# Expert tiles of a mixture-of-experts stage: one of each expert, then pairs on one load of weights, then singles, with the sums in two tables

## The chip, the cores and the metric

The kernel runs on one core of one Trainium2 chip. The metric is the time of one execution on the device, in microseconds (us). Three runs of the kernel before took 2542.0, 2550.27 and 2550.65 us; their median is 2550.27 us.

## What is computed

Two graph-attention stages and two feed-forward stages are run in turn on 3125 rows of 256 numbers, each with a layer norm in front and a residual behind it. The change lies in the second one, a mixture of 16 experts of which every row uses two, and at the border to the third, three graph-attention layers:

```python
def _L0_ffn_ref(x, gate_w, gate_b, w1, w2, w3):
    logits = jnp.einsum('bsd,de->bse', x, gate_w) + gate_b
    probs = jax.nn.softmax(logits, axis=-1)
    top_probs, top_idx = jax.lax.top_k(probs, 2)
    top_probs = top_probs / jnp.sum(top_probs, axis=-1, keepdims=True)
    dispatch = jnp.sum(jax.nn.one_hot(top_idx, n_experts, dtype=x.dtype) * top_probs[..., None], axis=-2)
    h1 = jnp.einsum('bsd,edh->bseh', x, w1)
    h2 = jnp.einsum('bsd,edh->bseh', x, w2)
    hidden = jax.nn.silu(h1) * h2
    expert_out = jnp.einsum('bseh,eho->bseo', hidden, w3)
    return jnp.einsum('bseo,bse->bso', expert_out, dispatch)
...
x = x + _L0_gnn_ref(_layernorm(x, axis=-1), ...)
x = x + _L0_ffn_ref(_layernorm(x, axis=-1)[None], ...)[0]
x = x + _L1_gnn_ref(_layernorm(x, axis=-1), ...)
x = x + _L1_ffn_ref(_layernorm(x, axis=-1)[None], ...)[0]
```

Here the model width is 256, an expert's hidden width is 512, and all of it is float32.

## The kernel before

Rows are held in 25 blocks of 128 (`NB`), and five blocks make a chunk (`NCH` is 5). The program is written with a framework that places instructions on each engine's queue by a model of its own, takes care of all waits, and hands out buffers from pools; where the source opens a `manual_schedule`, an engine keeps the written order. Each engine works through its own queue in order. DMAs are issued from the queues of SP, ACT and POOL.

**First graph layer (L550 to L719).** For each chunk and head, ACT and DVE make the choice matrices `t`, `m` and `m2` (L577 to L589) and PE multiplies them with the features (L593). They lie in the pool `m0` together with smaller tiles such as `red`, `total` and `gate_w`. At its end the residual rows are written to a table `x_d` in HBM and the normalised rows to `xn_d`.

**Routing (L736 to L958).** The gate's logits are made by PE, and DVE finds each row's two experts. From L858 on, DVE works in written order: `running` (L870) forms running sums by doubling steps, `pre` the rows of each expert before each block. From these come the number of 128-row tiles per expert, the expert of each tile (`owner`, L898), and every row's `place`. The two gate weights of each row are written as 8-byte pieces into `xn_d` by ACT (L924). One-hot matrices `slot`, `give` (L934, L939) and 2 x 25 matmuls into `pslot` (L942) turn places into lists: `token` (L955), the row number of each slot, and `target` (L958), where its result goes.

**Experts (L960 to L1019).** The 56 tiles (`MU`) of up to 128 rows are run one after the other, in the order of the experts. For each tile SP reads the tile's expert into a register (L967) and loads that expert's `w1`, `w2` and `w3` of 512 KB each (L976, L978, L980; six buffers each). POOL gathers the rows `xg` from `xn_d` (L982); PE transposes them (`pt`, L136) and ACT copies them (`xT`, L138); PE makes `h1` and `h2` (L991), ACT the silu (L995), DVE the product `hid` (L996), PE the output `po` (L999), DVE the weighted `yo` (L1005, three buffers). POOL then adds `yo` into the rows `target` of `x_d` with an indirect DMA (L1006). Ahead of the fifth tile `later_weights` (L830) loads the next layers' attention vectors on ACT's queue (L839) and DVE multiplies them in (L844). If the routing needs more than 56 tiles, branches behind the loop (L1014, L1017) run the rest. Then ACT loads the five chunks of `x` back from `x_d` (L1021).

**Start of the next graph layer (L1025 to L1139), called the feed below.** POOL loads `wr`, `br`, `fw1`, `fw2`, `fb2` and `b1r`, the bias of the last stage (L1102), which PE transposes (L1104) and DVE copies (L1105). `lengths` (L1112) makes the statistics of a chunk on DVE and ACT (L1117 to L1126); then each block is normalised (`rows`, L1134), transposed and multiplied by the layer's weights (`ph`, L1089, copied by ACT, L1090). Three layers follow that stream all pairs of nodes through ACT, DVE and PE (L1325, L1327, L1336).

Of the kernel before, what the change touches and what calls it, by code (L numbers as in the profile page):

```python
# [9 lines left out]
F32 = mybir.dt.float32  # L10
I32 = mybir.dt.int32
BF16 = mybir.dt.bfloat16
AF = mybir.ActivationFunctionType
OP = mybir.AluOpType
AX = mybir.AxisListType
PSUM = bass.MemoryType.PSUM

P = 128
N = 3125
NB = 25  # L20
NP = NB * P
# [16 lines left out]
MT = 64  # L38
MU = 2 * N // P + NE // 2
# [45 lines left out]
def network(ctx: ExitStack, tc: tile.TileContext, ins, out, flag):  # L85
# [10 lines left out]
    x_d = nc.dram_tensor("x_d", (NP + P, D), F32, kind="Internal").ap()  # L96

# [452 lines left out]
    with tc.tile_pool(name="m0a", bufs=1) as ap, tc.tile_pool(name="m0", bufs=2) as mp, tc.tile_pool(  # L550
# [21 lines left out]
        def produce(dc, h, s, state):  # L572
            if s == 0:
                state["row"] = heads.pop(0) if heads else head_row(dc, h)
            row, k = state["row"], s % CH
            at = tiles[dc, s // CH]
            if k == 2:  # L577
                m = mp.tile([P, CW], BF16, name="m", bufs=2)
                nc.vector.scalar_tensor_tensor(m, row, nleft[:, s, h : h + 1], at[:, k, :], op0=OP.is_ge, op1=OP.mult)  # L579
                return m  # L580

            if k in (0, 3):
                state["t"] = mp.tile([P, 2, CW], BF16, name="t")
                state["m"] = mp.tile([P, 2, CW], BF16, name="m2", bufs=3)
            t, m, i = state["t"], state["m"], k in (1, 4)
            nc.scalar.activation(t[:, int(i), :], row, AF.Relu, bias=steep[:, s, h : h + 1], scale=STEEP)  # L586
            if i:
                nc.vector.tensor_tensor(m, t, at[:, k - 1 : k + 1, :], OP.min)  # L588
            return m[:, int(i), :]  # L589
# [200 lines left out]
        with tc.manual_schedule(engines={mybir.EngineType.DVE, mybir.EngineType.Activation}):  # L790
# [7 lines left out]
            for b in range(NB):  # L798
# [4 lines left out]
                xt = mp.tile([P, 2, CW], BF16, name="t").rearrange("p k t -> p (k t)").bitcast(F32)  # L803
# [46 lines left out]
    with tc.tile_pool(name="mo", bufs=1) as mo:  # L850
        owner = mo.tile([P, MT], I32, name="owner")
        used = mo.tile([P, 1], I32, name="used")
# [5 lines left out]
        with tc.tile_pool(name="mg", bufs=1) as mg, tc.tile_pool(name="mg1", bufs=1, space=PSUM) as ps1, tc.manual_schedule(  # L858
# [3 lines left out]
            nc.sync.dma_start(x_d[NP:, :], clear)  # L862

# [6 lines left out]
            def running(tot, a, bb, n):  # L870
# [3 lines left out]
                while step < n:  # L874
# [7 lines left out]
            fullt = mg.tile([P, NE], F32, name="fullt")  # L882
            nc.vector.tensor_scalar(fullt, pre[:, NB - 1, :], float(P - 1), None, op0=OP.add)
            tiles_i = mg.tile([P, NE], I32, name="tiles_i")
            nc.vector.tensor_copy(tiles_i, fullt)
            nc.vector.tensor_scalar(tiles_i, tiles_i, 7, None, op0=OP.arith_shift_right)
            tiles = mg.tile([P, NE], F32, name="tiles")
            nc.vector.tensor_copy(tiles, tiles_i)
            end = running(tiles, mg.tile([P, NE], F32, name="end0"), mg.tile([P, NE], F32, name="end1"), NE)

            nc.vector.tensor_copy(used, end[:, NE - 1 :])
            which = mg.tile([P, MT, NE], F32, name="which")
            nc.gpsimd.iota(which, pattern=[[1, MT], [0, NE]], base=0, channel_multiplier=0,
                           allow_small_or_imprecise_dtypes=True)
            nc.vector.tensor_tensor(which, which, end[:, None, :].to_broadcast([P, MT, NE]), OP.is_ge)
            own = mg.tile([P, MT], F32, name="own")
            nc.vector.tensor_reduce(own, which, AX.X, OP.add)
            nc.vector.tensor_scalar(owner, own, float(NE - 1), None, op0=OP.min)  # L898

            base = mg.tile([P, NE], F32, name="base")  # L900
            nc.vector.tensor_sub(base, end, tiles)
            nc.vector.tensor_scalar(base, base, float(P), None, op0=OP.mult)
# [3 lines left out]
            nc.vector.tensor_add(where, where, base[:, None, :].to_broadcast(ex3))  # L906
# [22 lines left out]
            for i in range(2):  # L929
# [11 lines left out]
                for b in range(NB):  # L941
                    nc.tensor.matmul(pslot, hot[0][:, b // 2, :, b % 2], give[:, b // 2, :, :, b % 2],  # L942
                                     start=(i == 0 and b == 0), stop=(i == 1 and b == NB - 1))
            second = mg.tile([P, MT], F32, name="second")
# [15 lines left out]
        def experts(first, last, ew, deep):  # L960

            with tc.tile_pool(name="ep", bufs=2, space=PSUM) as ps:
                w3_loads = []
                for i in range(first, last):
                    if first == 0 and i == 4:
                        later_weights(ew, busy)
                    loads, (e,) = nc.values_load_multi_w_load_instructions(  # L967
                        owner[0:1, i : i + 1], engines=[mybir.EngineType.SP], min_val=0, max_val=NE - 1)
                    if i >= first + 2:

                        tc.add_manual_dep(
                            loads[0].ins, w3_loads[i - first - 2].ins.name,
                            mybir.DependencyInfo(mybir.DependencyClass.NoSync, mybir.DependencyReason.SCHED_ONLY),
                            reason="registers")
# [5 lines left out]
                    w3_loads.append(nc.sync.dma_start(w3, ins["L0_ffn_w3"][ds(e, 1)].rearrange("o (k p) h -> p (o k) h", p=P)))  # L980
                    xg = ew.tile([P, D + 2], F32, name="xg", bufs=6)
                    nc.gpsimd.indirect_dma_start(  # L982
                        out=xg, out_offset=None, in_=xn_d,
                        in_offset=bass.IndirectOffsetOnAxis(ap=token[:, i : i + 1], axis=0))
                    xt = transposed(ps, ew, xg)
                    hs = []
                    for w, name in ((w1, "h1"), (w2, "h2")):
                        ph = ps.tile([P, HID // P, P], F32, name=name)
                        for f in range(HID // P):
                            for k in range(2):  # L990
                                nc.tensor.matmul(ph[:, f, :], w[:, k, f * P : (f + 1) * P], xt[:, k, :],  # L991
                                                 start=(k == 0), stop=(k == 1))
                        hs.append(ph)
                    hid = ew.tile([P, HID // P, P], F32, name="hid")
                    busy = nc.scalar.activation(hid, hs[0], AF.Silu)  # L995
                    nc.vector.tensor_mul(hid, hid, hs[1])  # L996
                    po = ps.tile([P, D], F32, name="po")
                    for f in range(HID // P):
                        nc.tensor.matmul(po, hid[:, f, :], w3[:, f, :], start=(f == 0), stop=(f == HID // P - 1))  # L999
                    share = ew.tile([P, 1], F32, name="share")  # L1000
                    nc.vector.tensor_mul(share, xg[:, D + 1 :], turn[1][:, i : i + 1])  # L1001
                    nc.vector.scalar_tensor_tensor(share, xg[:, D : D + 1], turn[0][:, i : i + 1], share,
                                                   op0=OP.mult, op1=OP.add)
                    yo = ew.tile([P, D], F32, name="yo")
                    nc.vector.tensor_scalar(yo, po, share, None, op0=OP.mult)  # L1005
                    nc.gpsimd.indirect_dma_start(  # L1006
                        out=x_d, out_offset=bass.IndirectOffsetOnAxis(ap=target[:, i : i + 1], axis=0),
                        in_=yo, in_offset=None, compute_op=OP.add)


        experts(0, MU, ew0, 6)
        early.close()
        count = nc.values_load(used[0:1, 0:1], min_val=0, max_val=MT)
        with tc.If(count > MU):  # L1014
            with tc.tile_pool(name="ew2", bufs=2) as ew:
                experts(MU, MU + 2, ew, 2)
            with tc.If(count > MU + 2):  # L1017
                with tc.tile_pool(name="ew3", bufs=3) as ew:
                    experts(MU + 2, MT, ew, 3)  # L1019
        for g in range(NCH):  # L1020
            nc.scalar.dma_start(x[:, g * CH : (g + 1) * CH, :],  # L1021
                                x_d[g * CW : (g + 1) * CW, :].rearrange("(b p) c -> p b c", p=P))
# [52 lines left out]
    with tc.tile_pool(name="g1", bufs=1) as g1, tc.tile_pool(name="g1w", bufs=2) as gw, tc.tile_pool(  # L1075
# [24 lines left out]

        b1r = gw.tile([P, NP - CW], BF16, name="rjunk").bitcast(F32)[:NF, :P]
        nc.gpsimd.dma_start(b1r, ins["L1_ffn_b1"].rearrange("(f p) -> f p", p=P))  # L1102
        pr = ps.tile([P, 512], F32, name="ph")
        nc.tensor.transpose(pr[:, :NF], b1r, ident[:NF, :NF])  # L1104
        nc.vector.tensor_copy(fb1, pr[:, :NF])  # L1105
# [177 lines left out]
        with tc.tile_pool(name="g1l", bufs=3) as gm:  # L1283
            for layer in range(3):
# [17 lines left out]
                nc.vector.tensor_scalar(bp, q, SLOPE - 1.0, -HALF, op0=OP.mult, op1=OP.add)  # L1302
                cola = gw.tile([P, NB], F32, name="cola")
# [862 lines left out]
```

## Time and profile before

| | |
|---|---|
| median of 3 runs | 2550.27 us |
| profiled execution | 2551.61 us |
| its span, first to last instruction | 2549.8 us |
| mean granted PE clock | 0.919 |
| busy: PE, DVE, ACT, POOL | 87%, 61%, 50%, 8% |
| moved by DMA | 260.80 MB, mean 102 GB/s |
| first gather of the experts' loop starts | 1049.96 us |
| last `po` of the loop ends | 1417.0 us |
| first `ph` of the next layer | 1448.76 us |

Times on the page are counted from the first instruction. PE is the matrix engine, PEld its weight loads, DVE the vector engine, ACT the scalar engine, POOL the engine that issues indirect DMAs, SP the engine that issues most plain ones; a trailing q (SPq, ACTq) marks work of an engine's instruction queue, such as issuing a DMA. "out<-in" are the tiles that an instruction writes and reads, "xN" counts instructions, and a bracket at the end of a line gives the time the engine stood idle before it and what ended that. The granted clock is a share of full speed. An operation in float32 on PE appears as several instructions, so a tile has 32 of L991 and 8 of L999.

### The profile page before, as it was taken

The numbers are of one execution on the slowest core, as the hardware profiler recorded it, in microseconds if no ns is written. First come the engines' busy times: TensorE is split into PE (matmuls) and PEld (weight loads), VectorE is DVE, ScalarE is ACT, GpSimd is POOL, SyncE is SP. The second block draws the span as 40 slices with busy tenths as digits, with TensorE's granted clock in tenths as the row PEclk, the third lists the DMA queues.
The fourth block names the chain that finished last, engine by engine and source line by source line (L and its number), as shares of the span: only waits on it lengthen the run. The fifth ranks groups of instructions, "written<-read, shape, count | busy, mean of one in ns | idle before, by whom it ended". The sixth has DMA issues, their size and how long they took to land.

```text
span 2549.8 us, 38337 instructions
## 1 busy us (share of the span) xinstructions
PE 2207.5 (87%) x15049; PEld 1881.4 (74%) x15049; DVE 1543.5 (61%) x2932; ACT 1286.1 (50%) x1802; POOL 194.0 (8%) x182
## 2 busy tenths in 40 slices
PE   2516689999999999499999489999899998999997
PEld 1415568888888888488888368888788887888855
DVE  6699979999999996432222244444344443677861
ACT  1364479999999894011111154444444444444321
POOL 2000000000000000233443100000000000000021
PEclk9755599999999997699999699999999999999999
DMA  3006430202020211799997312222222221444230
GB/s 87 12 16 195 132 113 22 93 26 92 22 97 22 66 43 42 250 305 302 292 288 224 100 52 78 70 70 83 62 65 81 77 71 57 109 109 96 68 84 18
DMA packets 155516, 260.80 MB, mean 102 GB/s; under 512 B 12907, under 2 KB 99450, under 8 KB 155322
## 3 DMA queue, kind: packets, MB, share of 16 engines
q1 hardware_dynamic: 123939, 211.11, 26.4%
q0 software_dynamic: 13440, 22.80, 4.3%
q10 hardware_dynamic: 17942, 24.30, 3.5%
q8 instruction: 123, 2.02, 0.3%
q14 instruction: 72, 0.58, 0.1%
HBM read 211.60 MB, written 46.57 MB: 101 GB/s over the span
## 4 chain that ended last, share of the span: by engine, by line
PE 45%; DMA 10%; DVE 7%; ACT 2%; issue 2%; POOL 0%; ACTq 0%; DVEq 0%; POOLq 0%
PE bcc L1336 29%; DMA x_d<-yo,target 8%; PE ph L1089 3%; PE h L991 2%; PE acc L593 2%; PE bcc L1395 2%; PE po L999 1%; PE bcc L1388 1%; PE all L612 1%; DVE r L1327 1%; DVE rjunk L1198 1%; PE acc L807 1%; PE pt L136 1%; DVE yo L1005 1%; DMA xn_d<-x 1%
## 5 line engine op out<-in xcount | busy, mean ns | idle before, releaser
L1336 PE MATMUL bcc<-hx,r 128*128 128x257 f32 x3750 | 840.4, 383 | 13.4 <-DVE r L1327 13.4
L1336 PEld LDWEIGHTS bcc<-hx,r 128*128 128x128 f32 x3750 | 711.1, 191 | 113.2 <-DVE r L1327 13.7
L586 ACT ACTIVATE t<-row,steep 128x640 bf16<-128x640 f32 x800 | 592.4, 816 | 60.0 <-DVE m L588 39.1
L593 PE MATMUL acc<-parts,m 128*128 128x198 bf16 x5000 | 575.3, 247 | 5.8 <-DVE m L588 4.9
L1327 DVE SCALAR_TENSOR_TENSOR r<-t,colc,at 128x640 f32<-128x640 f32 x375 | 329.3, 882 | 398.4 <-PE bcc L1336 384.8
L1325 ACT ACTIVATE t<-rowb,colm,cola 128x640 f32<-128x640 f32 x375 | 341.9, 919 | 387.2 <-DVE r L1327 386.9
L593 PEld LDWEIGHTS <-m 128*128 128x128 bf16 x5000 | 442.1, 96 | 102.9 <-DVE m L588 18.1
L612 PE MATMUL all<-parts,at 128*128 128x396 bf16 x1250 | 365.2, 335 | 6.8 <-DVE total L614 4.5
L588 DVE TENSOR_TENSOR m<-t,at 128x1280 bf16<-128x1280 bf16 x400 | 326.3, 818 | 39.7 <-ACT t L586 31.9
L991 PEld LDWEIGHTS h<-xT,w 128*128 128x128 f32 x1792 | 214.1, 194 | 17.1 <-ACT xT L138 13.9
L991 PE MATMUL h<-xT,w 128*128 128x128 f32 x1792 | 218.8, 279 | 7.7 <-ACT xT L138 6.2
L529 PE MATMUL pa<-oh,ol 128*128 128x100 bf16 (+1 forms) x1120 | 94.7, 277 | 111.9 <-DVE oh L522 111.9
L579 DVE SCALAR_TENSOR_TENSOR m<-row,nleft,at 128x640 bf16<-128x640 f32 x200 | 174.2, 872 | 10.5 <-DMA adj<-cnt 8.1
L529 PEld LDWEIGHTS <-ol 128*128 128x128 bf16 x1120 | 87.0, 141 | 119.5 <-DVE oh L522 62.0
L995 ACT ACTIVATE hid<-h 128x512 f32<-128x512 f32 x56 | 33.4, 597 | 260.2 <-PE h L991 260.2
L1005 DVE TENSOR_SCALAR yo<-po,share 128x256 f32<-128x256 f32 x56 | 27.1, 484 | 196.3 <-DMA x_d<-yo,target 128.1
L612 PEld LDWEIGHTS <-at 128*128 128x128 bf16 x1250 | 118.9, 97 | 16.2 <-issue 10.0
L999 PE MATMUL po<-w,hid 128*128 128x256 f32 x448 | 113.9, 399 | 18.8 <-DVE hid L996 18.8
L138 ACT COPY xT<-pt 128x256 f32<-128x256 f32 x158 | 55.9, 374 | 118.1 <-PE pt L136 113.9
L532 ACT CAST cnt<-pa 128x2000 bf16<-128x2000 f32 x40 | 73.0, 1825 | 82.8 <-PE pa L529 82.8
L999 PEld LDWEIGHTS po<-w,hid 128*128 128x128 f32 x448 | 82.5, 194 | 35.1 <-DVE hid L996 21.9
L1006 POOL DMA_INDIRECT x_d<-yo,target x56 | 89.1, 1591 | 210.3 <-DVE share L1001 118.5
(405 smaller groups left out, 1748.3 us busy)
## 6 DMA issues: line engine op xcount, KB each, us to landing
w<-in_L_ffn_w_dram SPq DMA_DIRECT2D x168, 512.0 KB
at<-adj SPq DMA_DIRECT2D x100, 800.0 KB
adj<-cnt SPq DMA_DIRECT2D x10, 2000.0 KB
row<-er_d ACTq DMA_DIRECT2D x40, 320.0 KB
xf_d<-hx SPq DMA_DIRECT2D x5, 1282.5 KB
right<-rr_d ACTq DMA_DIRECT2D x15, 320.0 KB
x_d<-x SPq DMA_DIRECT2D x5, 640.0 KB
xn_d<-at SPq DMA_DIRECT2D x5, 640.0 KB
```

Source lines behind the costliest of these rows:

```text
L529: nc.tensor.matmul(pa[:, q // NW, p0 + c0 : p0 + c1], hot[0][:, q // 2, :, q % 2], hot[1][:, q // 2, c0:c1, q % 2], start=(u == 0), stop=( ...
L579: nc.vector.scalar_tensor_tensor(m, row, nleft[:, s, h : h + 1], at[:, k, :], op0=OP.is_ge, op1=OP.mult)
L586: nc.scalar.activation(t[:, int(i), :], row, AF.Relu, bias=steep[:, s, h : h + 1], scale=STEEP)
L588: nc.vector.tensor_tensor(m, t, at[:, k - 1 : k + 1, :], OP.min)
L593: nc.tensor.matmul(acc[:, db // 2, db % 2 * C6 : (db % 2 + 1) * C6], m[:, db * P : (db + 1) * P], parts[:, s, h, :], start=(s == 0 and db ...
L612: nc.tensor.matmul(alone, at, parts[:, s, hs, 3 * C1 :], start=(s == 0), stop=(s == NB - 1))
L991: nc.tensor.matmul(ph[:, f, :], w[:, k, f * P : (f + 1) * P], xt[:, k, :], start=(k == 0), stop=(k == 1))
L999: nc.tensor.matmul(po, hid[:, f, :], w3[:, f, :], start=(f == 0), stop=(f == HID // P - 1))
L1006: nc.gpsimd.indirect_dma_start(out=x_d, out_offset=bass.IndirectOffsetOnAxis(ap=target[:, i : i + 1], axis=0), in_=yo, in_offset=None, com ...
L1325: nc.scalar.activation(t, rowb[:, dw], AF.Relu, bias=colm[:, s : s + 1], scale=cola[:, s : s + 1])
L1327: nc.vector.scalar_tensor_tensor(r, t, colc[:, s : s + 1], at[:, s % CH, :], op0=OP.add, op1=OP.mult)
L1336: nc.tensor.matmul(accs[dc][db][:, : D + 1], r[:, db * P : (db + 1) * P], hx[:, s, : D + 1], start=(s == 0), stop=(s == NB - 1))
```

## The change

- Tiles of experts: every expert gets a first tile, whose expert is known when the program is built (`alone`). What an expert has beyond 128 rows is cut into pairs of tiles, which load the weights once (`pair`), and at most one single tile (`single`). The loop always runs 16 first tiles, 17 pairs (PU) and 6 singles (SU), first tiles and pairs in turn; two branches behind it run 7 more pairs and 10 more singles if the routing needs them. There are 80 slots (MT) for 64.
- The places of the rows are worked out for this order, with more operations on DVE; `owner` (now one entry for each pair and single) is worked out after the matmuls into `pslot`.
- The scatters go in turn to `z_d` and `x_d`. `z_d` is zeroed from SP before the loop; after it both tables are loaded and added.
- The choice matrices `t`, `m`, `m2` get a pool of their own (`m0`; the other tiles are in `m0b`).
- The last stage's bias `b1r` is loaded and transposed at the start of the second graph layer of the three.

```diff
-MT = 64
-MU = 2 * N // P + NE // 2
+PAIRS = (2 * N // P - NE) // 2 + 8
+MT = NE + 2 * PAIRS + NE
+PU = (2 * N // P - NE) // 2 + 1
+SU = NE // 2 - 2
...
-    with tc.tile_pool(name="m0a", bufs=1) as ap, tc.tile_pool(name="m0", bufs=2) as mp, tc.tile_pool(
+    with tc.tile_pool(name="m0a", bufs=1) as ap, tc.tile_pool(name="m0b", bufs=2) as mp, tc.tile_pool(
+        name="m0", bufs=2) as mc, tc.tile_pool(
...
-                m = mp.tile([P, CW], BF16, name="m", bufs=2)
+                m = mc.tile([P, CW], BF16, name="m", bufs=2)
...
+            nc.sync.dma_start(z_d.rearrange("(b p) c -> p b c", p=P), clear[:, None, :].to_broadcast([P, NB + 1, D]))
+            ce = mg.tile([P, NE], F32, name="ce")
+            nc.gpsimd.iota(ce, pattern=[[P, NE]], base=0, channel_multiplier=0, allow_small_or_imprecise_dtypes=True)
...
+            rest = mg.tile([P, NE], F32, name="rest")
+            nc.vector.tensor_scalar(rest, pre[:, NB - 1, :], -1.0, 0.0, op0=OP.add, op1=OP.max)
...
+            nc.vector.tensor_scalar(more_i[:, :, 0], rest_i, 8, None, op0=OP.arith_shift_right)
+            nc.vector.tensor_scalar(more_i[:, :, 1], rest_i, 7, None, op0=OP.arith_shift_right)
+            nc.vector.tensor_scalar(more_i[:, :, 1], more_i[:, :, 1], 1, None, op0=OP.bitwise_and)
+            more = mg.tile([P, NE, 2], F32, name="more")
+            nc.vector.tensor_copy(more, more_i)
+            end = running(more, mg.tile([P, NE, 2], F32, name="end0"), mg.tile([P, NE, 2], F32, name="end1"), NE)
...
             nc.vector.tensor_sub(where, pre, ptot)
             nc.vector.tensor_add(where, where, pin)
-            nc.vector.tensor_add(where, where, base[:, None, :].to_broadcast(ex3))
+            shift = mg.tile(ex3, F32, name="shift")
+            nc.vector.scalar_tensor_tensor(shift, where, float(P), wide(pairs_from), op0=OP.is_ge, op1=OP.mult)
+            nc.vector.tensor_tensor(t3, where, wide(first_behind), OP.is_ge)
+            nc.vector.tensor_mul(t3, t3, wide(behind_pairs))
+            nc.vector.tensor_add(shift, shift, t3)
+            nc.vector.tensor_add(where, where, wide(ce))
+            nc.vector.tensor_add(where, where, shift)
...
+            nc.vector.tensor_copy(used, end[:, NE - 1, :])
+            which = mg.tile([P, PAIRS + NE, NE], F32, name="which")
...
+            nc.vector.tensor_scalar(owner, own, float(NE - 1), None, op0=OP.min)
...
+        def alone(e):
+            return None, e, [e]
+
+        def pair(j):
+            return owner[0:1, j : j + 1], None, [NE + 2 * j, NE + 2 * j + 1]
+
+        def single(j):
+            return owner[0:1, PAIRS + j : PAIRS + j + 1], None, [NE + 2 * PAIRS + j]
...
+                for g, (of, e, tiles) in enumerate(groups):
+                    if first and g == 4:
+                        later_weights(ew, busy)
+                    if of is not None:
+                        loads, (e,) = nc.values_load_multi_w_load_instructions(
+                            of, engines=[mybir.EngineType.SP], min_val=0, max_val=NE - 1)
...
                     w1 = ew.tile([P, 2, HID], F32, name="w1", bufs=deep)
                     nc.sync.dma_start(w1, ins["L0_ffn_w1"][ds(e, 1)].rearrange("o (k p) h -> p (o k) h", p=P))
...
+                    for i in tiles:
+                        xg = ew.tile([P, D + 2], F32, name="xg", bufs=6)
...
+                        gave[0] += 1
+                        nc.gpsimd.indirect_dma_start(
+                            out=(x_d, z_d)[gave[0] % 2],
+                            out_offset=bass.IndirectOffsetOnAxis(ap=target[:, i : i + 1], axis=0),
+                            in_=yo, in_offset=None, compute_op=OP.add)
...
-        experts(0, MU, ew0, 6)
+        groups = []
+        for k in range(NE):
+            groups.append(alone(k))
+            if k < PU:
+                groups.append(pair(k))
+        groups += [pair(j) for j in range(NE, PU)] + [single(j) for j in range(SU)]
+        experts(groups, ew0, 6, first=True)
...
+        with tc.If(count > PU):
+            with tc.tile_pool(name="ew2", bufs=2) as ew:
+                experts([pair(j) for j in range(PU, PAIRS)], ew, 2)
+        count = nc.values_load(used[0:1, 1:2], min_val=0, max_val=NE)
+        with tc.If(count > SU):
+            with tc.tile_pool(name="ew3", bufs=3) as ew:
+                experts([single(j) for j in range(SU, NE)], ew, 3)
+        with tc.tile_pool(name="zt", bufs=2) as zp:
+            for g in range(NCH):
+                xs, zt = x[:, g * CH : (g + 1) * CH, :], zp.tile([P, CH, D], F32, name="zt")
+                for t, d in ((xs, x_d), (zt, z_d)):
+                    nc.scalar.dma_start(t, d[g * CW : (g + 1) * CW, :].rearrange("(b p) c -> p b c", p=P))
+                nc.vector.tensor_add(xs, xs, zt)
...
-        b1r = gw.tile([P, NP - CW], BF16, name="rjunk").bitcast(F32)[:NF, :P]
-        nc.gpsimd.dma_start(b1r, ins["L1_ffn_b1"].rearrange("(f p) -> f p", p=P))
-        pr = ps.tile([P, 512], F32, name="ph")
-        nc.tensor.transpose(pr[:, :NF], b1r, ident[:NF, :NF])
-        nc.vector.tensor_copy(fb1, pr[:, :NF])
...
+                if layer == 1:
+                    b1r = gw.tile([P, NP - CW], BF16, name="rjunk").bitcast(F32)[:NF, :P]
+                    nc.gpsimd.dma_start(b1r, ins["L1_ffn_b1"].rearrange("(f p) -> f p", p=P))
...
```

## The prediction

> **What bounds the kernel now.** The page's chain that ended last puts 8% of the span on `x_d<-yo,target`, the accumulating scatter of the experts' outputs. Its 40 slices show the only long stretch of full DMA (300 GB/s) in slices 16 to 21, the experts' loop, so I read that stretch, 1020 to 1500 us, by the chain in order of time, the table of windows, the waits, and then the timeline.
>
> The windows (us, busy time of PE, PEld, DVE, ACT, POOL with instructions, granted clock, DMA share, GB/s):
>
> ```profile
> 1130.00:1180.00 50.00, 45.38 (x321) 41.73 (x320) 11.60 (x31) 7.36 (x16) 17.20 (x13) 0.97 0.98 313
> 1280.00:1330.00 50.00, 44.87 (x327) 41.31 (x326) 12.03 (x32) 7.45 (x16) 18.51 (x14) 1.00 0.98 291
> 1380.00:1400.00 20.00, 19.70 (x143) 18.37 (x142) 4.93 (x13) 2.44 (x5) 8.46 (x7) 1.00 0.41 81
> ```
>
> Two things are nearly full at once: DMA 0.98 and PE about 0.9. Once the weights are in (last row) PE is at 0.985 and DMA at 0.41. PE is the floor; what keeps it off the floor is in the waits of 1050 to 1400:
>
> ```profile
> DVE yo L1005 <- DMA x_d<-yo,target: 128.1, 28, 7.8
> ```
>
> (us in total, times, longest), and the chain (start, us, what):
>
> ```profile
> 1218.75 6.01 DMA x_d<-yo,target
> 1224.86 0.49 DVE yo L1005
> 1225.53 4.62 DMA x_d<-yo,target
> 1230.25 0.49 DVE yo L1005
> 1230.92 6.12 DMA x_d<-yo,target
> ```
>
> Every scatter waits until the one before it has landed (all add into `x_d`). Three `yo` buffers fill, then DVE stands at `yo`, behind it the product `hid` of the next tile, behind that PE. One such stall, by engine:
>
> ```profile
> 1169.41 0.49 PE L991 MATMUL h<-xT,w 128*128 128x128 f32 x2 [0.30 <-DMA at<-adj]
> 1171.75 0.48 DVE L1005 TENSOR_SCALAR yo<-po,share 128x256 f32<-128x256 f32 x1 [7.80 <-DMA x_d<-yo,target]
> 1172.60 0.68 DVE L996 TENSOR_TENSOR hid<-hid,h 128x512 f32<-128x512 f32 x1
> 1173.33 3.15 PE L999 MATMUL po<-w,hid 128*128 128x256 f32 x8 [3.43 <-DVE hid L996]
> ```
>
> The pace shows it. The third products (`po`, L999) start at 1098.52 and, eleven tiles on, at 1164.01: 5.95 us a tile, with DMA at 0.98, so full queues alone don't slow PE. From 1191.07 to 1243.55 eight scatters follow each other at 6.56 us. That excess is the loss. After the loop:
>
> ```profile
> 1425.98 3.96 ACTq L1021 DMA_DIRECT2D x<-x_d  x5
> 1432.65 0.57 POOL L1102 DMA_DIRECT2D rjunk<-in_L_ffn_b_dram  x1
> 1445.41 0.24 PE L1104 MATMUL ph<-ident,rjunk 8*128 8x8 f32 x1 [28.40 <-DMA rjunk<-in_L_ffn_b_dram]
> 1445.69 0.17 DVE L1105 COPY fb<-ph 128x8 f32<-128x8 f32 x1 [11.58 <-PE ph L1104]
> ```
>
> A 4 KB load of a bias, needed only in the last stage, queues behind 2.3 MB on POOL's queue; DVE's copy of it stands in front of the layer norm's reciprocal, whose input was ready at 1435.9.
>
> **Do the tiles fit?** Both kernels execute 56 tiles without a branch (L991 is x1792, 32 a tile). The reference's routing gives the experts 250, 178, 1365, 332, 681, 836, 159, 102, 323, 209, 65, 377, 837, 32, 482 and 22 rows: 16 first tiles, 17 pairs, 6 singles. PU is 17 and SU is 6: it fits with nothing to spare. Weights are loaded 16+17+6 = 39 times for 56, 61 MB for 88.
>
> **Part 1, fewer weight loads: 0 us by themselves.** PE does the same 56 x 42 matmuls, and at 5.95 us a tile it did so under a full DMA. What the smaller traffic could give is the step from 5.95 to the 5.89 us a tile of 1379.66 to 1415.02: 3 us, kept for the range.
>
> **Part 2, two tables: -18.9 us.** `po` starts run from 1064.67 (tile 0) to 1415.02 (tile 55): 350.35 us. Without scatter stalls: 55 x 5.95 = 327.3, less 0.9 for the first three steps (16.96 as measured), plus 5.0 for the attention vectors' loads and products (L839, L844: the two steps from 1081.63 to 1098.52 took 16.9 us), which stay: 331.4. Each table now gets a scatter every 11.9 us and needs 6.56; POOL's own work is 0.99 + 1.59 us a tile (rows L982, L1006). Next late is PE itself.
>
> **Part 3, the routing before the loop: +2 us.** The first gather (L982) started at 1049.96, when both the gates' write (issued 1034.50, landed 14.66 us later) and the token list (1048.2) were there. On DVE, in written order: from the running sum to `place` 7.0 us go (1023.58 to 1030.57); in come 13 small operations at 0.2, nine of a running sum (1.4, as L872 to L876) and eight 400 wide at 0.6: 8.8, so +1.8. The lists are 80 wide for 64: six operations 1664 wide become 2080 wide, 0.98 to 1.23 us each, +1.5; the second 25 `pslot` matmuls 2.83 to 3.5, +0.7. Token list: 1052.2. `which`, `own`, `owner` (2 us) now lie in the 2.9 us in which DVE waited for `pslot`; without that cover they are +2. The gates' write is issued at 1036.3 and by its row lands at 1051.0, before the list. So the gather is 2.5 us later. Against that, the first expert's number is a constant, so weights for single first tiles can load before the routing is known; a gather on a quieter DMA lands nearer the 3.9 us of the last scatter than its own 6. I take +2, ends -1 and +5. `z_d`'s zeroing (3.4 MB from SP at about 1015, 11 us at 313 GB/s) is over before its first scatter near 1069; SP's weights stand behind it, with 30 us in hand. The pairs' owners come at 1050 for 1028, and SP loads a group (5 us) faster than PE uses one (39 groups in 333 us, 8.5).
>
> **Part 4, after the loop: -7.3 us.** Before, the last `po` ended at 1417.0 and the last scatter waited for two others; `x` loads began at 1425.98. Now: 0.6 to the issue, 3.9 to land (1420.97 to 1424.9), 0.8 for POOL's counting past the branch, then a second branch on POOL, by the first one's row 2.3 (1420.8 to 1421.8, 0.5 of semaphores, 0.77 of counting), 0.35: 8.0 for 9.0, -1.0. Each group now needs two loads and an add. ACT issues ten. First group: 5.3 us from issue to the first statistics as before, plus 640 KB at the 320 GB/s of 1430 to 1445, 2.0 (0 if the two loads overlap freely), plus the add, 1.48 (row L266, 128x1280 f32): +3.5. The bias load leaves this place: the reciprocal at 1435.95 for 1445.77, -9.8; in layer 1 its transpose and copy lie beside `cola` and `colc` on ACT: 0, at most 0.6. The Trainium skill (DMA: Bandwidth & Descriptors, Issuing engines are not separate DMA queues) says that transfers of all queues share the same 16 engines, so by it the second table's read-back cannot run beside the first's for nothing; by that rule the sum is as it stands, and without it 2 us lower. No run here has shown it yet.
>
> The other four adds (5.9 us) fall in a stage where DVE is busy 26 of 60 us: I take +1.5. The third to fifth `z` loads wait for a buffer, that is for an add, and in ACT's queue the square roots (L1119) and copies of the feed may stand behind them: 0 to +7, I take +1.
>
> **The pool of its own:** m, t and m2 keep their buffer counts: 0, within 1 either way.
>
> **Sum:** +2 - 18.9 - 7.3 + 1.5 + 1 = -21.7 us. The profiled execution took 2551.6 (span 2549.8 and 1.8 around it), 1.3 above the median 2550.3 of the three runs. Against the median: 2528.6, so 2528.5. Ends of this case: loop -27 (L839's stall and the 3 us gone too), start -1, tail -8: 2514; loop -14, start +5, tail -2: 2539.
>
> **Rivals.** *Scatters still queue.* Both tables are served by one POOL in order, and if a scatter into one table were held by the other's landing, 18.9 us would stay: -3, 2547. For it: POOL itself waited 43.9 us in 12 places for a landing. Against it: those were all of the same table. Chance 0.08.
> *The read-back holds the feed.* All ten loads stand in ACT's queue before L1119, so the feed starts when the third group is summed, some 30 us after the last `po`, as before: tail +1.5, total -13 to -15, 2536 to 2538. Chance 0.08, half on each side of the bound below.
> *Slower: the handover between tiles breaks.* Now PE does the next tile's `h` while ACT and DVE make `hid`. The groups change the order in which instructions are put on PE. Where a tile is not overlapped, PE waits for the silu (0.60), the product (0.69), the transposes and copy (1.1) and signals: about 2.5 us. Nine such places cancel the forecast; at each of 17 pairs it is +43, total +21, 2571. Against it: two PSUM buffers and the dependencies of a tile are unchanged, and weights come early. Chance 0.08.
> *The tiles don't fit:* with a seventh single ten more tiles run, 60 us and 10 for unfetched weights, 2598. The nearest count is 7 rows from a bound. Chance 0.02.
>
> **Numbers.** The forecast has 0.74, of which 0.03 falls short of the bound. I call 0.5% (12.8 us) what a measurement of this kernel tells from no change: faster 0.71 + 0.04 = 0.75; same 0.03 + 0.04 + 0.08 = 0.15; slower 0.10. The range goes from 2513 to 2549, which leaves out the two slower cases and the fringes.
>
> **What would show it.** Right: `yo` no longer waits for a landing; `po` starts 5.9 to 6.0 us apart throughout; first `pt` near 1058 (1056.1), last `po` ending near 1400; the feed's first `ph` some 25 us after it for 32; no DVE wait for L1105's copy; the first-tile weights issued before 1029. Wrong: gaps at `po` waiting for `hid` that remain, a gap before pairs ending with `w`, the feed's first copies late behind `z` loads, or over 56 tiles.

## The result and the profile after

The changed kernel takes 2526.41 us (median of four runs, 2522.7 to 2528.98), the kernel before 2547.25 us beside it: a ratio of 0.9919, 95% interval 0.9895 to 0.9943, so 20.8 us less. A second set of runs gave 0.9910 (0.9893 to 0.9928). The forecast was 2528.5. The profiled execution took 2527.2 (span 2525.4), 24.4 below the profiled one of before.

The loop's windows after (same columns as those shown of before):

```profile
1180.00:1230.00 50.00, 48.81 (x354) 45.26 (x353) 13.24 (x33) 7.36 (x16) 20.75 (x16) 1.00 0.81 233
1280.00:1330.00 50.00, 48.23 (x350) 44.65 (x348) 13.24 (x33) 8.01 (x18) 22.38 (x18) 1.00 0.78 220
```

PE is at 0.97 for 0.9, DMA at 0.8 for 0.98. The waits from 1045 to 1400 us (us in total, times, longest) have no `yo` that waits for a landing any more:

```profile
DVE yo L1050 <- PE po L1044: 102.1, 47, 3.9
POOL x_d L1052 <- DMA z_d<-yo,target: 8.9, 5, 3.9
```

The second line, five POOL waits that are put down to the other table's landing, is not in the second profile of the same kernel, and PE's steps show no loss from it. The `po` starts (now L1044) run from 1055.49 to 1387.54, 332.05 us for 350.35, in steps of 5.73 and 6.09 in turn. One stall is left, at the attention vectors' products: two steps of 11.07 and 8.10.

After the loop (timeline: start, us, engine, line, what, idle time before and its end):

```profile
1396.97 0.38 ACTq L1077 DMA_DIRECT2D x<-x_d  x1
...
1405.00 1.49 DVE L1078 TENSOR_TENSOR x<-x,zt 128x1280 f32<-128x1280 f32 x1 [6.81 <-DMA zt<-z_d]
...
1409.10 0.18 DVE L1168 BATCH_NORM_AGGREGATE mv<-ln_st 128x2 f32<-128x6 f32 x1
...
1413.92 0.37 ACTq L1077 DMA_DIRECT2D zt<-z_d  x1
1414.32 1.28 ACT L1169 ACT_TABLE_LOAD   x1 [28.79 <-DMA x<-x_d]
...
1416.15 1.49 DVE L1078 TENSOR_TENSOR x<-x,zt 128x1280 f32<-128x1280 f32 x1 [2.25 <-DMA zt<-z_d]
1417.56 0.18 DVE L1171 RECIPROCAL rstd<-rstd 128x5 f32<-128x5 f32 x1
1419.82 1.49 DVE L1078 TENSOR_TENSOR x<-x,zt 128x1280 f32<-128x1280 f32 x1 [2.08 <-DMA zt<-z_d]
...
1423.58 0.80 DVE L1184 TENSOR_SCALAR rows<-x,mv,ss 128x256 f32<-128x256 f32 x2
```

The bias copy no longer stands here, and yet the first `rows` come 34 us after the last `po`. The square root of the first group (L1169) stands in ACT's queue behind the last `z` load, which waits for a buffer, that is for an add; and from there on DVE has the fourth and fifth adds among the steps of the first group's layer norm: between them stands one reciprocal (L1171), and the rest follows the fifth.

Cut at the same events, the two executions and those of the experiments differ as follows (us; `x_d`: start of the last write of `x_d` in the first graph layer; loop: first to last tile's first `po`; tail: last `po`'s end to the feed's first `ph`; feed: from there to the first `bcc`):

| kernel | `x_d` | to first `po` | loop | tail | feed | rest |
|---|---|---|---|---|---|---|
| before | 991.3 | 73.4 | 350.4 | 31.8 | 58.1 | 1042.9 |
| changed | 982.1 | 73.3 | 332.1 | 36.1 | 56.8 | 1043.0 |
| changed, again | 983.9 | 75.5 | 330.9 | 36.3 | 52.7 | 1042.5 |
| pool undone | 989.5 | 74.4 | 331.6 | 36.0 | 57.3 | 1044.2 |
| pool only | 981.7 | 66.2 | 354.1 | 31.5 | 58.1 | 1043.2 |
| tables only | 988.2 | 73.7 | 330.5 | 33.5 | 57.2 | 1042.3 |
| bias only | 987.8 | 73.6 | 349.8 | 23.1 | 52.4 | 1040.6 |
| one table | 983.2 | 68.3 | 337.1 | 26.2 | 52.8 | 1041.2 |
| one table, again | 980.4 | 73.9 | 332.2 | 20.6 | 52.2 | 1042.5 |

From before to changed: -9.1, 0, -18.3, +4.4, -1.3, 0. So the loop did what was forecast, the tail did not, and a gain in a layer far ahead of the loop took its place. Single executions differ too: with the shared pool the last write of `x_d` lies between 988 and 991 us.

### The profile page after: what moved, and what is told of

It is laid out like the page before. It is cut to its first block, busy times and chain, and to the rows that moved or that the text cites. A ratio compares the mean times of both kernels' runs of the same rounds, so it can differ in the third digit from the quotient of the medians.

```text
span 2525.4 us, 37965 instructions
## 1 busy us (share of the span) xinstructions
PE 2190.7 (87%) x15049; PEld 1875.5 (74%) x15049; DVE 1557.9 (62%) x2950; ACT 1285.1 (51%) x1802; POOL 193.4 (8%) x184
## 5 line engine op out<-in xcount | busy, mean ns | idle before, releaser
L618 PE MATMUL all<-parts,at 128*128 128x396 bf16 x1250 | 372.2, 336 | 6.9 <-DVE total L620 4.6
L1044 PE MATMUL po<-w,hid 128*128 128x256 f32 x448 | 110.7, 391 | 5.9 <-DVE hid L1041 5.9
L1041 DVE TENSOR_TENSOR hid<-hid,h 128x512 f32<-128x512 f32 x56 | 38.5, 687 | 120.1 <-PE h L1036 118.0
L1145 PE MATMUL ph<-w,xT 128*128 128x258 f32 x300 | 86.1, 411 | 13.2 <-ACT xT L143 7.7
```

Of the source, the lines that this page charges most:

```text
L618: nc.tensor.matmul(alone, at, parts[:, s, hs, 3 * C1 :], start=(s == 0), stop=(s == NB - 1))
L1145: nc.tensor.matmul(ph[:, : D + 2], xt[:, k, :], weights[layer][:, k, :], start=(k == 0), stop=(k == 1))
```

## The experiments

Each ratio is to the kernel before, beside it on the same chip, with its 95% interval.

**The pool, undone and alone.** Two kernels: the changed one with the choice matrices in the shared pool again, and the one before with only that part done.

```diff
-tc.tile_pool(name="m0", bufs=2) as mp
+tc.tile_pool(name="m0b", bufs=2) as mp, tc.tile_pool(name="m0", bufs=2) as mc
...
-m = mp.tile([P, CW], BF16, name="m", bufs=2)
+m = mc.tile([P, CW], BF16, name="m", bufs=2)
```

(and likewise for `t` and `m2`; undone, the other way round)

> The changed kernel with one part undone: the choice matrices m, t and m2 of the first graph layer take their memory from the shared pool again; two tables, groups and the bias move stay. Theory: the 9.1 us by which the first graph layer now ends earlier (its last write of x_d at 982.15 for 991.27) come from the pool alone, since the shared pool's buffers lay over the adjacency builder's cnt, and the first m and t had to wait until cnt was written out (8.05 and 8.66 us in the profile before). Then this kernel shows both waits again (8 to 9 us at about 332 us of the span), its last x_d write lies near 991, and it takes 8 to 9 us more than the changed kernel: about 2535. Rival (the prediction's term: the pool is worth 0 within 1): the same time as the changed kernel, 2526, and no such wait.

> The kernel before with one part done: the choice matrices of the first graph layer in a pool of their own. Theory (they lay over cnt, and the first m and t waited 8.1 and 8.7 us for its writes): both waits are gone, the last write of x_d is issued at 982 to 984 for 987.8 to 991.3 with the shared pool, and the kernel takes 6 to 9 us less than before, about 2537. Rival (the prediction's 0): the wait is gone, but PE, which needed the first t and m no earlier, ends the layer at the same time, and the time stays within 2 us of 2545.

Undone: 2533.66 us, 0.9938 (0.9918 to 0.9958). Alone: 2538.64 us, 0.9972 (0.9962 to 0.9983), some 7 us less than before. The timeline of before at the start of the first graph layer:

```profile
332.45 1.68 DVE L579 SCALAR_TENSOR_TENSOR m<-row,nleft,at 128x640 bf16<-128x640 f32 x2 [8.05 <-DMA adj<-cnt]
332.68 13.06 ACT L586 ACTIVATE t<-row,steep 128x640 bf16<-128x640 f32 x18 [8.66 <-DMA adj<-cnt]
```

and the waits from 320 to 345 us with the pool undone:

```profile
ACT t L591 <- DMA adj<-cnt: 8.7, 1, 8.7
DVE m L584 <- DMA adj<-cnt: 8.1, 1, 8.1
```

Neither `m` nor `t` reads `cnt` or `adj`; they wait for `cnt` to be written out, as they would if their buffers lay in its memory (the addresses themselves were not read). With a pool of their own, with or without the rest of the change, no such wait is in the trace, and the last `x_d` write comes at 980 to 984 us, for 988 to 991 in every kernel with the shared pool. The theory holds. In single medians the undone kernel's interval overlaps the changed one's; the pool alone against before is what settles it.

**One table or two, 39 weight loads or 56.** The changed kernel without the second table (no `z_d`, no zeroing, no read-back), and the kernel before with the second table alone:

```diff
-out=(x_d, z_d)[gave[0] % 2],
+out=x_d,
...
-nc.vector.tensor_add(xs, xs, zt)
```
```diff
-out=x_d, out_offset=bass.IndirectOffsetOnAxis(ap=target[:, i : i + 1], axis=0),
+out=(z_d, x_d)[i % 2],
+out_offset=bass.IndirectOffsetOnAxis(ap=target[:, i : i + 1], axis=0),
```

> The changed kernel with one part undone: all scatters add into x_d, there is no z_d, no zeroing of it, no second load and no add after the loop; the groups, the fewer weight loads, the pool and the bias move stay. Theory (the scatter chain is what the two tables took away): the loop's po starts run over about 350 us for 332, DVE's yo waits again for the landing of x_d<-yo,target, some 120 us in 28 places; after the loop 10 to 13 us come back (no z loads: the feed's first ph some 24 us after the last po for 36.1); in all 5 to 8 us slower than the changed kernel, 2531 to 2534. Rival (the fewer weights are what freed the chain: with 39 loads for 56 DMA is quieter and a scatter lands in about 4.5 us for 6.56, less than the 5.9 us of a tile): the loop stays near 332 and the kernel is 10 to 13 us faster than the changed one, about 2514.

> The kernel before with one part done: scatters alternate between x_d and z_d, z_d is zeroed, and both are loaded and added after the loop as in the changed kernel; one weight load for each tile, the old order of tiles, the shared pool and the bias load before the layer norm stay. Theory (the scatter chain is the loop's loss, whatever the weights): no wait of yo for a landing is left, po starts run over 331 to 334 us for 350.35, and with the longer tail (+10 to +13) the total is 5 to 9 us below the kernel before. Rival (the fewer weight loads made the loop faster): under full DMA the scatters of two tables still queue, po starts run over 345 or more, and the total is 5 to 12 us above the kernel before.

One table: 2512.94 us, 0.9873 (0.9857 to 0.9889), faster than the changed kernel; again, 2512.73, 0.9888 (0.9866 to 0.9909). Tables only: 2528.48 us, 0.9926 (0.9910 to 0.9941). A loop window of tables only, and the waits of the two one-table executions:

```profile
1180.00:1230.00 50.00, 48.80 (x356) 45.41 (x355) 13.43 (x35) 7.36 (x16) 22.24 (x19) 1.00 1.04 328
```
```profile
DVE yo L1048 <- DMA x_d<-yo,target: 134.7, 36, 5.8
```
```profile
DVE yo L1048 <- PE po L1042: 91.4, 42, 3.9
POOL x_d L1050 <- DMA x_d<-yo,target: 72.9, 20, 8.2
...
DVE yo L1048 <- DMA x_d<-yo,target: 30.1, 10, 4.2
```

The first row shows PE as busy as in the changed kernel beside a DMA share of 1.04: with two tables, full queues cost the loop nothing, as the prediction had read from one stretch. The others show that with 39 loads the one table is no longer much of a bound either, although `yo` still waits for landings. Its scatters follow each other, from 1150 to 1360 us, at a median of 6.7 us with 56 loads (6.53 in bias only), and of 6.16 and 5.59 in the two executions with 39; a tile takes PE 5.91. So the loops are, with one and with two tables: 350.4 and 330.5 at 56 loads, 337.1 or 332.2 and 332.1 or 330.9 at 39. Either cure alone does most of it; with both, the second table still saves 0 to 6 us in the loop. It costs 10 to 15 us behind it (tail 36.1 for 26.2 or 20.6). In the first execution the waits were those of the theory (134.7 us in 36 places for some 120 in 28), but the loop was 337.1 us and not 350; in the second, waits and loop were the rival's, and the total was the rival's in both. No run changes the number of loads alone: the one-table kernel has the new order of tiles as well.

Tables only had the loop that its theory gave (no wait of `yo` for a landing, 330.5 us), but it came out some 17 us under the kernel before, for 5 to 9 forecast: its tail grew by 1.7 us and not by 10 to 13. PE transposes the bias there at 1409.7 us, and the first `rows` come at 1426.2, behind the fifth add, so the read-back took the place of the wait for the bias instead of adding to it.

The repeat also had a question of its own:

> The one-table kernel again, beside the kernel ahead of it on the same chip: 2511 to 2516. If its early first ptot (21.0 us behind the last write of x_d, for 27 to 28 in the changed kernel) was the granted clock of that execution (0.82 between 976 and 1000 us of the span) and not the missing zeroing of z_d, it is 27 to 28 wherever the clock there is 0.5 to 0.6, and the span is then some 6 us longer than the first run's 2510.8; if it was the zeroing, it is 21 again at any clock.

The first `ptot` came 27.8 us behind the last `x_d` write at a clock of 0.50 (976 to 1000 us), as in the changed kernel at 0.53. The other executions bear this out: where the clock falls to 0.50 some 8 us behind that write, `ptot` comes after 21 us (the first one-table execution, and pool only); 2 us behind it, after 23.4 (read at once, which zeroes `z_d`); 3 to 5 us ahead of it, after 27 to 28, with the zeroing and without. So the 21.0 was the clock, and the zeroing of `z_d` costs nothing that shows. The other half of the expectation failed: the span was 2503.8 us, 7.0 shorter and not 6 longer, since loop and tail gave back 4.9 and 5.6 us. In the first execution two scatters still stood in line behind the last `po`, which is its longer tail.

**The bias alone.**

```diff
-b1r = gw.tile([P, NP - CW], BF16, name="rjunk").bitcast(F32)[:NF, :P]
...
+if layer == 1:
+    b1r = gw.tile([P, NP - CW], BF16, name="rjunk").bitcast(F32)[:NF, :P]
```

> The kernel before with one part done: the bias load of the last stage, its transpose and its copy moved from ahead of the layer norm into the second layer; all else as before. Theory (the prediction's term): the layer norm's reciprocal was ready at 1435.9 and ran at 1445.8 behind the copy, so 9.8 us less, about 2537. Rival: another wait takes its place, such as the rows of group 0 behind the x loads in ACT's queue, and the time stays within 2 us of the kernel before, 2545 to 2549.

2533.26 us, 0.9958 (0.9943 to 0.9973), 11 us less. The timeline after its loop:

```profile
1423.19 4.11 ACTq L1021 DMA_DIRECT2D x<-x_d  x5
...
1434.29 0.73 DVE L1128 TENSOR_SCALAR rows<-x,mv,ss 128x256 f32<-128x256 f32 x2
```

From the loads to `rows` 11.1 us, for 21.1 before (1425.98 to 1447.08): 10.0 gained, 9.8 forecast. The term was right; in the changed kernel the read-back stands where the bias stood.

**The read-back done otherwise.** The second table is loaded into memory that the second layer uses later, so that no load waits for a buffer, and each group is added at the head of its own layer norm; first with the `z` loads on SP and `x` on ACT, then all ten on SP in the order of use:

```diff
+zs = hxs[1].rearrange("p b h -> p (b h)")[:, : NB * D].rearrange("p (b c) -> p b c", c=D)
+for g in range(NCH):
+    for t, d in ((x, x_d), (zs, z_d)):
+        nc.sync.dma_start(t[:, g * CH : (g + 1) * CH, :], ...
...
 def lengths(g):
+    nc.vector.tensor_add(x[:, gs, :], x[:, gs, :], zs[:, gs, :])
```

> The changed kernel with the second table's read-back done in another way: its five loads go from SP at once into memory that the second layer uses later (so none waits for a buffer, and none stands in ACT's queue ahead of the square root), and each add stands at the head of its own group's layer norm. Theory (in the changed kernel the feed waited behind the third to fifth z loads in ACT's queue, square root at 1414.3, rows at 1423.6): from the first x load to the feed's first ph it takes some 17 us (13.2 as with one table, 1.5 for the add, 2 for 640 KB more) for 28.7, so last po end to first ph is about 25 for 36.1, and the kernel is 8 to 12 us faster than the changed one, about 2516, and some 0 to 5 us faster than the one-table kernel's 2513 only if the rest of the feed keeps its pace. Rival (the bytes themselves are the price: 6.6 MB must be read for 3.3): the first ph comes no earlier than 1422 in the span, and the kernel stays within 4 us of the changed one.

> The changed kernel itself, beside the others on the same chip: 2522 to 2529. With the clock of TensorE between 976 and 1000 us of the span as low as before (0.53), the first product ptot comes 27 to 28 us after the last write of x_d; if it is granted as in the one-table kernel (0.82), 21.

> The kernel with the read-back at once, but all ten loads in one queue, SP's, in the order of use: x and z of the first group, x and z of the second, and so on. In the kernel before it the x and z loads stood in two queues and the first z landed 16 us after its issue (1394.2 to 1410.1), behind bytes of x that were not needed yet. Theory (the second table costs where its bytes stand in the queues): x and z of the first group, 1.28 MB at 350 GB/s, land 6 us after the first issue, the first ph follows some 16 us after the first issue, 23 to 25 us after the last po's end (36.1 in the changed kernel, 33.7 with two queues, 26.2 with one table); with the loop's 5 us that is 2507 to 2512, the same as one table or up to 5 us better. Rival (the bytes are the price in any order: 6.6 MB beside POOL's 2.3 MB take 25 us, and the feed, group by group, runs no faster than they come): the first ph comes early, but the first bcc stays 86 or more us behind the last po's end (92.9 in the changed kernel, 79.0 with one table), and the time stays at 2518 or more.

On SP at once: 2522.66 us, 0.9908 (0.9896 to 0.9921); the changed kernel beside it 2524.66. In turn: 2523.72, 0.9916 (0.9893 to 0.9939). Neither gain is more than the runs can tell; in time the rivals were right both times. Tails: 33.8 and 28.9 us for 36.1 (the first `ph` at 1419.5 and 1419.2, earlier than the first rival allowed). The order did bring the feed's start 7 us nearer to the loop's end; but from the first `ph` to the first `bcc` the kernel in turn then took 63.6 us, so that `bcc` began 92.5 us behind the loop, as the second rival had it. In the changed kernel again, the first `ptot` came 27.8 us behind the last `x_d` write at a clock of 0.57. The timeline in turn:

```profile
1397.62 0.38 SPq L1134 DMA_DIRECT2D x<-x_d  x1
1398.95 0.37 SPq L1134 DMA_DIRECT2D hx<-z_d  x1
...
1409.85 1.49 DVE L1163 TENSOR_TENSOR x<-x,hx 128x1280 f32<-128x1280 f32 x1 [8.76 <-DMA hx<-z_d]
```

The first `z` lands 10.9 us after its issue, though it stands second in its queue: at 274 GB/s some 3.0 MB moved in that time, and the first `x` and `z` are 1.3 MB of it. The rest are later loads of the queue and POOL's weights for the last stage.

To part the bytes from the adds, two more kernels, one without the adds, and one without the `z` loads and with adds of another operand (both leave the second table's sums out of `x`):

```diff
-    nc.vector.tensor_add(x[:, gs, :], x[:, gs, :], zs[:, gs, :])
```
```diff
-    nc.vector.tensor_add(x[:, gs, :], x[:, gs, :], zs[:, gs, :])
+    nc.vector.tensor_add(x[:, gs, :], x[:, gs, :], x[:, gs, :])
```

> The kernel with all ten loads in turn on SP, without the five adds: z is still loaded, and not added, so the second table's sums are missing from x. Theory (the bytes of the second table hold the feed): from the last po's end to the first ph about 26 to 28 us (28.9 with the adds), first bcc still 86 to 92 us behind the last po's end, and the time within 3 us of the kernel with the adds, 2521 to 2524. Rival (the adds on DVE hold it, five of 1.49 us between a group's arrival and its statistics): the first bcc comes 75 to 80 us behind the last po's end, and the time is about 2513.

> The same kernel without the five loads of z: each add takes x twice (so x is doubled, and the second table's sums are missing). Theory (the bytes hold the feed): the first ph comes 20 to 23 us behind the last po's end, the first bcc 75 to 81 us behind it as with one table (72.9 and 79.0), and the time is 2510 to 2515. Rival (the adds hold it): the first bcc stays 86 or more us behind the last po's end, and the time is 2520 or more.

Loads only: 2513.19 us, 0.9869 (0.9840 to 0.9897), tail 20.5. Adds only: 2515.61, 0.9882 (0.9856 to 0.9909), tail 22.0. So the bytes that nobody waits for cost nothing (tail 20.6 with one table, in its second execution), the first add costs its 1.5 us, and both together cost 8.3: nearly 7 us of it is the wait of the first add for the first `z`. The theory that the bytes by themselves hold the feed fell with the loads alone, and the rival, that the adds do, with the adds alone.

What sets the 63.6 us of the kernel in turn apart from the 55.1 of the read-at-once kernel, which has its adds in the same place, is the clock. PE in the feed, in turn (first row) and with one table (second), with the same columns as the windows above:

```profile
1426.00:1444.00 18.00, 15.44 (x38) 9.83 (x39) 7.67 (x25) 4.64 (x14) 0.00 (x0) 0.50 0.15 46
```
```profile
1426.00:1444.00 18.00, 14.92 (x66) 10.07 (x66) 12.91 (x54) 8.42 (x30) 0.00 (x0) 1.00 0.12 38
```

38 matmuls for 66 in the same busy time, at half the granted clock. The clock, 0.50 since shortly after the loop's end, comes back to 1.00 within 5 us of the first `ph` (one table twice, bias only, the changed kernel again, read at once, products later: feed 52 to 55 us), after 16 to 19 us (before, changed, pool undone, pool only, tables only, loads only, adds only: 57 to 59) or after 26 us (in turn: 63.6). The second rival's 86 us and more came true this way, and not by the bytes. The changed kernel is in the first set in one execution and in the second in the other, so the second table does not decide it. What does, and how often each occurs, the single profiles cannot tell; it stays open.

**The products later.** The read-at-once kernel with the products of the attention vectors written eight groups behind their loads.

```diff
 if first and g == 4:
     later_weights(ew, busy)
+if first and g == 12:
+    later_products()
```

> The kernel before this one in the list, with one more step: the products of the later layers' attention vectors stand eight groups later than their loads, so that DVE need not wait for the loads. Theory: the two steps from the fifth to the seventh po, 19.2 us in the changed kernel for 11.8 of two tiles, fall to 13 to 15 (the products themselves are 12 of 0.35 us on DVE), the po starts run over 326 to 328 us for 332, and the time is 4 to 6 us below the kernel before it. Rival: the stall only moves to where the products now stand, or is a wait for the experts' own weights, and the time is the same within 2 us.

2523.49 us, 0.9919 (0.9906 to 0.9932), no change, and the two steps are 10.50 and 8.18. The trace shows that the edit didn't do what it says: DVE still runs the products from 1085.51 to 1093.5 us, right behind their loads, since its order here is planned and not the text's. Whether the stall can be removed is left open.

## Why the prediction was right, and where its steps failed

The total (-21.7 forecast, -20.8 in medians, -24.4 in the profile) was right with two steps wrong by about 9 us each, against each other: that they cancelled is luck.

- **Two tables, -18.9.** Measured -18.3, for the reason given: no `yo` waits for a landing, and the steps are 5.91 us on average for the 5.95 assumed. The stall at the attention vectors took 19.2 us for two tiles where 16.9 was carried over, which ate the gain per tile.
- **Fewer weight loads, 0.** True beside two tables (330.5 at 56 loads, 330.9 and 332.1 at 39). As a statement "by themselves" it was wrong: with one table they are worth 13 to 18 us, together with the new order of tiles. Scatters then follow each other sooner (6.16 or 5.59 us for 6.5 to 6.7), at a DMA share of about 0.8 for 0.98; that the quieter DMA is the reason is argued and not shown. The sum could not show that, because it gave the whole stall to the tables.
- **Routing, +2.** From the last `x_d` write to the first gather 58.7 and 58.9 us: +0.2. From the running sum to the token list it was +1.9 for +4.0; of that the 80-wide operations and the second `pslot` gave +0.4 for 2.2, as the second 25 matmuls took 1.95 us instead of the 3.5 assumed. That was the clock and not the sum: they ran at 1.00, while the first 25, at about 0.50, took 3.49, as did both sets in pool undone, where the first gather came 59.6 us after the last `x_d` write. As forecast, the gates' write is no longer what the gather waits for.
- **The pool, 0 within 1.** This failed: -9.1 in the profile (up to 3 of it the spread between executions), -7 in medians. The step counted buffers and did not ask where they lie. The page of before held the line in its costliest groups, `m` with 8.1 us of idle time ended by `adj<-cnt`, a transfer that `m` does not read; I read no wait of this stage, since it lies 700 us ahead of the loop.
- **After the loop, -7.3, and the adds, +2.5.** This failed: +4.4 to the first `ph`. The bias term was right by itself (10.0 for 9.8). The first `z` landed 8.0 us after the first issue and its add followed, close to the +3.5 forecast for both. Mis-sized was the line "in ACT's queue the square roots may stand behind them: 0 to +7, I take +1". The square root came 5 us after its statistics, and then DVE had the fourth and fifth adds ahead of the rest, with waits of 2.25 and 2.08. The +1.5 for those adds counted their work and not these waits. From the first statistics to `rows` it took 17.1 us (1406.52 to 1423.58), for 5.9 in loads only: 11 us.
- **The rivals.** "The read-back holds the feed" came true in its mechanism (not the third group's add but the fifth's), and its 2536 to 2538 was missed mainly because the pool gave back 7 to 9 us: with the pool undone the time is 2533.7. No tile was held up by a scatter into the other table (steps of 5.73 and 6.09 outside the one stall), and the handover held in pairs and singles alike. The rule that the prediction took from the Trainium skill (DMA: Bandwidth & Descriptors, Issuing engines are not separate DMA queues) agrees with these runs where somebody waits: the first `z` landed 10.9 us after its issue beside the others. Where nobody waited, the same bytes cost nothing.

Best is the changed kernel without the second table: 2512.7 to 2512.9 us, 1.1 to 1.3% under the kernel before and some 9 us under the change (0.9873 and 0.9888 for 0.9919 and 0.9910).

## What to carry to other kernels

Two cures for one stall do not add: price each with the other in place, since the second may bring little and still cost its full read-back. When a wait names a transfer that the waiting instruction doesn't read, look for buffers that share memory; a pool of its own can be worth more than the edit under study. Of a read-back behind a loop, the bytes that nobody waits for cost nothing here; ask which load the first consumer waits for, and what stands ahead of it on each engine.

## What the runs showed of the hardware

Accumulating scatters of 128 rows that wait for each other followed at 4.4 to 4.6 us at the end of the loop before, when no weights are loaded any more, and at a median of 6.5 to 6.7 beside 56 tiles' loads at a DMA share of 0.98.

After the idle time behind the loop, the granted clock came back within 5 us of the first `ph` in six executions and took 16 to 26 in eight, with PE 86% busy at 0.50 in the longest. Each us more of half clock cost the feed about 0.4 us. The two executions of the changed kernel give 56.8 - 52.7 over 15.9 - 4.5, which is 0.36; the kernels in turn and read at once give 63.6 - 55.1 over 26.5 - 4.2, which is 0.38. The Trainium skill (TensorE: Matmul & The Clock Gate, Part 1: The HAM clock gate) has the full clock back after about 3.4 us of sustained work, in a window whose phase changes from run to run. The quick executions agree; the 16 to 26 us of the others do not, unless the feed's short gaps, 14% of the time in that stretch, count as no sustained work, which was not tried.
